# Layer 2's output gate computed ahead of its product, layer 3's first loads reordered, the last super chunk in halves

## The chip, the cores and the metric

The kernel runs on one core of one Trainium2 chip. The metric is the device time in microseconds (us) of the whole kernel, one launch, median of the runs shown. The engines are named as in the profile: PE is TensorE (matmuls), DVE is VectorE, ACT is ScalarE, POOL is GpSimd and SP is the engine whose queue issues nearly all DMAs here. All data are 32-bit floats; each fp32 matmul shows in the trace as two matmul records.

## The reference, cut to what matters

Four residual layers act on an image of 256 x 256 positions with 128 channels. Each is `x = x + layer(group_norm(x))`. Layer 0 is a triangle attention, layer 1 a triangle product with 16 channels; the change touches only layer 2 and the start of layer 3.

```python
# layer 2
zn = layernorm(z)                                   # over the 128 channels
a = sigmoid(zn @ Wga + bga) * (zn @ Wla + bla)
b = sigmoid(zn @ Wgb + bgb) * (zn @ Wlb + blb)
k = einsum('bimc,bmjc->bijc', a, b)                 # one 256 x 256 product per channel
out = sigmoid(zn @ Wgo + bgo) * (layernorm(k) @ Wlo + blo)
# layer 3: t is a 3x3 convolution of 128 channels to one
t = relu(conv(x, w1) + b1)
y = concat([x[:, :1], x[:, 1:] + t[:, :-1]], axis=1)
u = relu(conv(y, w1) + b1)
z = u + roll(y, 1, axis=1)                          # (two rows at the edge differ)
p = z, with relu(z @ w2c + b2) added, shifted along the width
q = relu(p @ w2c + b2) + p shifted                  # (two columns at the edge differ)
```

## The kernel before

Channels lie on the 128 partitions and the 65536 positions are cut into 32 super chunks (`NSC`) of 2048 (`SC`), each four matmuls wide (`CK` = 512). Between stages the data go through DRAM: `x2T` is layer 2's input, `aD` and `bD` are a and b, `kD` is k, `x3T` is layer 3's input. Layer 2 has three stages, and the code's names end in their numbers.

Stage 5 (lines 877 to 994) makes a and b. Per super chunk it runs 16 matmuls (`product5`, line 945), four sigmoids on ACT and four multiply-adds on DVE (line 976), and stores to `aD` and `bD`. The layer norm's factor is worked out a block of four super chunks at a time: `sums5` (PE), `root5`, a reciprocal, a store to `rs2D`, and `spread5`, which loads a row of `rs2D` broadcast over all partitions into `zns[s]`; `normalise5` then makes the normalised x there. The first block does this before the loop, with `fac` as its result (lines 950 to 962).

Stage 6 (lines 999 to 1054), the planes: `load6` loads four channels of a and b, `tri_turn` transposes (PE, then a copy on DVE), `tri_multiply` multiplies, and ACT, DVE and POOL copy the plane and keep its sum (`k1`) and sum of squares (`k2`). At the end `k1` and `k2` are turned into k's layer norm factor by three DVE steps, a square root on ACT and a reciprocal on DVE; the result goes through DRAM (`rkD`) to come back with one super chunk to a partition (`rk`). `rs2` is the same layout of stage 5's factor.

Stage 7 (lines 1057 to 1119), the output: `load7` loads k and x of a super chunk together, three ahead. `broadcast_rows` spreads a factor row over all partitions with four matmuls of 32 rows (line 860) into PSUM; `normalise_k` and `normalise_z` apply it on DVE, one super chunk ahead of use. Per half of a super chunk, `product7` makes the gate's matmuls and then those of k; ACT does the sigmoid, DVE the multiply-add. POOL adds the result to x for the whole super chunk (line 1116). `finish7` runs one super chunk later: two passes of ACT over x for the next group norm's sums (`g1`, `g2`) and the store to `x3T`.

Stage 9 (lines 1156 to 1419), layer 3: it works on chunks of 8 image rows (`load9`). The one-channel convolution goes round through DRAM: `taps` writes nine tap rows to `sD`, `load_block` loads them shifted (`p9_S`, for 16 rows), `sum_taps` makes t, `keep_t` stores it to `tD`, `load_t` loads it one row up, `image_u` and `image_e` make `e`, which goes to `eD` and back by `load_e` into `ers`. `finish_z` adds it to z. Two blocks, 0 and 1, are made before the loop; later ones are made inside it, a piece in each iteration. In an iteration, `p_half` and `q_half` are eight matmuls' worth of products with their DVE steps, and `emit` transposes and stores chunk s - 2.

Stages 5, 6, 7 and 9 stand under a manual schedule: the order on each engine is the order of the code. All DMAs of them but four are issued by SP, in the order of the code too; SP waits with an instruction until what it reads or overwrites is ready, and everything later on SP waits behind it. A tile pool that opens takes over memory of pools that were closed, and its first users wait for the last users of what lay there.

Of the kernel before, what the change touches and what calls it, by code (L numbers as in the profile page):

```python
# [15 lines left out]
P = 128  # L16
# [15 lines left out]
def kernel(ctx: ExitStack, tc: tile.TileContext, a: dict, out: bass.AP):  # L32
# [822 lines left out]
    def broadcast_rows(psX, rows, s, name):  # L855


        rb = [psX.tile([P, 2, CK], F32, name=name, tag="x") for _ in range(2)]
        for c in range(4):
            nc.tensor.matmul(  # L860
                rb[c // 2][:, c % 2, :], lhsT=sel[32 * c : 32 * c + 32, s : s + 1].to_broadcast([32, P]),
                rhs=rows[32 * c : 32 * c + 32, :], start=True, stop=True,
            )
        return [t.rearrange("p c t -> p (c t)") for t in rb]
# [5 lines left out]
    rs2_pool = rs2_scope.enter_context(tc.tile_pool(name="rs2", bufs=1))  # L870
    KB = 4
    BT = KB * SC
    with tc.tile_pool(name="p5", bufs=2) as sb, tc.tile_pool(name="p5psX", bufs=1, space=PSUM) as psX, tc.tile_pool(
# [4 lines left out]
        def load5(s):  # L878
            if s < NSC:
                xs[s] = sb.tile([P, SC], F32, name="p5_x", bufs=9)  # L880
                nc.sync.dma_start(xs[s], x2T[:, s * SC : (s + 1) * SC])
# [67 lines left out]

        for s in range(2 * KB):  # L950
            load5(s)
# [4 lines left out]
        fac = sb.tile([P, CK], F32, name="p5_fac", bufs=1)  # L956
        nc.vector.reciprocal(fac, var)
        store_block(rs2D, 0, fac)
        for s in range(2):
            spread5(s)  # L960
        normalise5(0)
        for s in range(NSC):
            b, j = divmod(s, KB)
            load5(s + 2 * KB)
# [26 lines left out]
            del zns[s]  # L991
            if j == 1 and (b + 1) * KB < NSC:
                compact5(b + 1, sums5(b + 1))


    rk = rs2_pool.tile([P, CK], F32, name="rk")
    rs2 = rs2_pool.tile([P, CK], F32, name="rs2_")
# [4 lines left out]
    with tc.tile_pool(name="p6", bufs=3) as sb, tc.tile_pool(name="p6s", bufs=1) as ssb, tc.tile_pool(  # L1002
        name="p6ps", bufs=3, space=PSUM
    ) as ps:
        k1 = ssb.tile([P, 2 * N], F32, name="p6_k1")
        k2 = ssb.tile([P, 2 * N], F32, name="p6_k2")
        nc.vector.memset(k1, 0.0)
        nc.gpsimd.memset(k2, 0.0)
        with tc.manual_schedule():
# [32 lines left out]

        nc.vector.scalar_tensor_tensor(k1, k1, -1.0 / D, k1, ALU.mult, ALU.mult)
        nc.vector.tensor_tensor(k2, k2, k1, ALU.add)
        nc.vector.tensor_scalar(k2, k2, 0.0, None, ALU.max)
        nc.scalar.activation(k2, k2, AF.Sqrt, bias=epst, scale=1.0 / D)
        nc.vector.reciprocal(k1, k2)
        nc.sync.dma_start(
            rkD.rearrange("o (p t) -> p (o t)", p=P), k1
        )  # L1050
        for c in range(4):
            nc.sync.dma_start(
                rk[32 * c : 32 * c + 32, :], rkD.rearrange("o (s c t) -> c (o s) t", c=4, t=CK)[c]
            )


    g1 = const.tile([P, NSC], F32, name="g1")
    g2 = const.tile([P, NSC], F32, name="g2")
    with tc.tile_pool(name="p7", bufs=2) as sb, tc.tile_pool(name="p7psX", bufs=2, space=PSUM) as psX, tc.tile_pool(
        name="p7psM", bufs=2, space=PSUM  # L1060
    ) as psM, tc.manual_schedule():
        ks, xs, kns, zns = {}, {}, {}, {}

        def load7(s):
            if s < NSC:
                ss = slice(s * SC, (s + 1) * SC)
                ks[s] = sb.tile([P, SC], F32, name="p7_k", bufs=4)
                nc.sync.dma_start(ks[s], kD[:, ss])
                xs[s] = sb.tile([P, SC], F32, name="p7_x", bufs=6)
                nc.sync.dma_start(xs[s], x2T[:, ss])  # L1070

        def normalise_k(s):
            rb = broadcast_rows(psX, rk, s, "p7_rk")
            kns[s] = sb.tile([P, SC], F32, name="p7_kn")
            for h in range(2):
                hs = slice(h * H2, (h + 1) * H2)
                nc.vector.tensor_tensor(kns[s][:, hs], rb[h], ks[s][:, hs], ALU.mult)
            del ks[s]

        def normalise_z(s):  # L1080
            rb = broadcast_rows(psX, rs2, s, "p7_rz")
            zns[s] = sb.tile([P, SC], F32, name="p7_zn")
            for h in range(2):
                hs = slice(h * H2, (h + 1) * H2)
                nc.vector.scalar_tensor_tensor(zns[s][:, hs], xs[s][:, hs], m2, rb[h], ALU.subtract, ALU.mult)

        def product7(src, w, h):
            pm = psM.tile([P, 2, CK], F32, name="p7_pm")
            for c in range(2):
                k = 2 * h + c  # L1090
                nc.tensor.matmul(pm[:, c, :], lhsT=w, rhs=src[:, k * CK : (k + 1) * CK], start=True, stop=True)  # L1091
            return pm.rearrange("p c t -> p (c t)")

        def finish7(s):
            junk = sb.tile([P, SC], F32, name="p7_j", bufs=1)
            nc.scalar.activation(junk, xs[s], AF.Identity, bias=m2neg, accum_out=g1[:, s : s + 1])
            nc.scalar.activation(junk, xs[s], AF.Square, bias=m2neg, accum_out=g2[:, s : s + 1])
            nc.sync.dma_start(x3T[:, s * SC : (s + 1) * SC], xs[s])
            del xs[s]

        for s in range(3):
            load7(s)
        normalise_k(0)
        normalise_z(0)
        for s in range(NSC):
            load7(s + 3)
            gt = sb.tile([P, SC], F32, name="p7_g")
            for h in range(2):
                hs = slice(h * H2, (h + 1) * H2)
                pg = product7(zns[s], wf2[:, 4, :], h)  # L1110
                nc.scalar.activation(gt[:, hs], pg, AF.Sigmoid, bias=b2w[:, 4:5])
                pl = product7(kns[s], w2c_[:, 5, :], h)
                nc.vector.scalar_tensor_tensor(gt[:, hs], pl, b2w[:, 5:6], gt[:, hs], ALU.add, ALU.mult)  # L1113
                if s + 1 < NSC:
                    (normalise_k if h else normalise_z)(s + 1)
            nc.gpsimd.tensor_tensor(xs[s], xs[s], gt, ALU.add)  # L1116
            if s:
                finish7(s - 1)
        finish7(NSC - 1)


# [41 lines left out]
    with tc.tile_pool(name="p9", bufs=2) as sb, tc.tile_pool(name="p9psM", bufs=2, space=PSUM) as psM, tc.tile_pool(  # L1163
# [167 lines left out]
        for s in range(2):  # L1331
            load9(s)
# [20 lines left out]
        for s in range(2, 4):  # L1353
            load9(s)
        sum_taps(-1)
        nc.sync.dma_start(image_rows(tD, 0, 1), blocks.pop(-1)["t"][P - 8 : P, 4 : 4 + BW])
        sum_taps(0)
        keep_t(0)
        load_t(0)
        image_u(0)  # L1360
        image_e(0)
        load_e(0)
        for s in range(2, 4):
            taps(xs[s], s * R, 4)
        load_block(1)
        for s in range(4, LEAD + 1):
            load9(s)
        finish_z(0)
        sum_taps(1)
        keep_t(1)  # L1370
        image_u(1)
        load_t(1)
        image_e(1)
        for s in range(4, LEAD):
            taps(xs[s], s * R, 4)
        load_e(1)
        load_block(2)
        load9(LEAD + 1)
        for s in range(NR + 2):
            load9(s + 8)  # L1380
            b = s // 2 + 2
            if s % 2 == 1 and b < NB:
                load_t(b)
            if s % 2 == 0 and 2 < b <= NB:
# [22 lines left out]
            if b < NB:  # L1407
# [6 lines left out]
            if s + LEAD < NR:  # L1414
                taps(xs[s + LEAD], (s + LEAD) * R, 4)
            if s % 2 == 1 and b + 1 < NB:
# [185 lines left out]
```

## Time and profile before

| what | us |
|---|---|
| median of 3 runs (3517.76 to 3522.11) | 3517.95 |
| the profiled execution's own time | 3521.85 |
| its span | 3520.2 |
| stage 5's loop, PE busy throughout | 492.7 |
| stage 6's loop, PE busy 290.95 of | 291.8 |
| stage 7's loop, PE busy 300.16 of | 300.4 |
| from the end of stage 7's loop to the ninth stage's third chunk | 81.2 |
| the rest of stage 9, PE busy 337.56 of | 357.0 |

The times are sums over windows of the trace, read at the points where the chain of waits changes stage. The profile is of one execution, so a difference between two kernels is made between two profiled executions, and the medians say how large the difference is. PE's busy time counts matmuls as the trace's model places them; a window that is busy throughout is one in which PE's order alone sets the pace.

Over the whole span PE is busy for 3123.1 us (89%), DVE for 2318.3, ACT for 1956.9 and POOL for 1611.1.

### The profile page before, as it was taken

The numbers are of one execution on the slowest core, as the hardware profiler recorded it, in microseconds if no ns is written. First come the engines' busy times: TensorE is split into PE (matmuls) and PEld (weight loads), VectorE is DVE, ScalarE is ACT, GpSimd is POOL, SyncE is SP. The second block draws the span as 40 slices with busy tenths as digits, with TensorE's granted clock in tenths as the row PEclk, the third lists the DMA queues.
The fourth block names the chain that finished last, engine by engine and source line by source line (L and its number), as shares of the span: only waits on it lengthen the run. The fifth ranks groups of instructions, "written<-read, shape, count | busy, mean of one in ns | idle before, by whom it ended". The sixth has DMA issues, their size and how long they took to land.

```text
span 3520.2 us, 52462 instructions
## 1 busy us (share of the span) xinstructions
PE 3123.1 (89%) x20268; PEld 1648.5 (47%) x20268; DVE 2318.3 (66%) x2638; ACT 1956.9 (56%) x2194; POOL 1611.1 (46%) x822
## 2 busy tenths in 40 slices
PE   4565999999999999965597899999999899949998
PEld 3512555555555555521432344443899433314444
DVE  4623888888888888852398354544555577737776
ACT  3563777777777777733243454443444366636655
POOL 4002777777777777732497000000555344414343
PEclk7887999999999999979798899999999899969999
DMA  9883333333333333349599586765999788647664
GB/s 333 322 304 123 98 121 110 110 122 112 107 122 115 105 121 115 108 162 380 175 342 343 224 314 249 278 262 197 351 350 350 291 333 336 263 167 204 194 193 136
DMA packets 309867, 760.54 MB, mean 216 GB/s; under 512 B 77627, under 2 KB 148957, under 8 KB 259181
## 3 DMA queue, kind: packets, MB, share of 16 engines
q1 hardware_dynamic: 298749, 747.48, 60.4%
q0 software_dynamic: 10864, 9.65, 0.9%
q8 instruction: 162, 2.65, 0.3%
q14 instruction: 92, 0.75, 0.1%
HBM read 469.33 MB, written 287.66 MB: 215 GB/s over the span
## 4 chain that ended last, share of the span: by engine, by line
PE 39%; DMA 7%; DVE 2%; ACT 1%; POOL 1%; SPq 1%; issue 0%; ACTq 0%; DVEq 0%; POOLq 0%
PE p_pm L945 13%; PE p_pm L1091 7%; PE tp_z L1560 6%; PE p_pm L1286 5%; PE tp_a L1549 2%; DMA p_x<-x1T 2%; DMA x2T<-p_x 1%; PE p_st L902 1%; PE p_pt L1323 1%; PE p_rz L860 1%; PE p_rk L860 1%; PE p_eb L860 1%; PE p_pp L1179 1%; PE p_pg L810 1%; POOL p_x L827 1%; DMA p_t<-tD 0%
## 5 line engine op out<-in xcount | busy, mean ns | idle before, releaser
L489 DVE TENSOR_TENSOR p_e<-p_S,triT 128x1024 f32<-128x1024 f32 x512 | 609.4, 1212 | 144.6 <-PE p_S L479 144.6
L499 POOL TENSOR_TENSOR p_es<-p_e 128x1024 f32<-128x1024 f32 x256 | 603.4, 2368 | 127.0 <-issue 67.2
L497 ACT ACTIVATE p_e<-p_e,mbT 128x1024 f32<-128x1024 f32 x512 | 551.9, 1138 | 63.1 <-DVE p_e L489 61.3
L945 PE MATMUL p_pm<-p_zn,wf 128*128 128x512 f32 x1024 | 444.3, 596 | 15.8 <-DVE p_zn L938 15.8
L464 PE MATMUL p_mm<-p_xn,wf 128*128 128x512 f32 x768 | 409.1, 617 | 9.2 <-POOL p_xn L437 9.2
L437 POOL TENSOR_TENSOR p_xn<-p_xn,p_rs 128x1024 f32<-128x1024 f32 x64 | 153.5, 2399 | 455.0 <-DMA p_x<-xT 262.7
L945 PEld LDWEIGHTS p_pm<-p_zn,wf 128*128 128x128 f32 x1024 | 194.9, 191 | 265.4 <-issue 244.8
L479 PE MATMUL p_S<-p_q,p_k 32*128 32x256 f32 x4096 | 295.4, 400 | 5.0 <-DVE p_e L489 5.0
L479 PEld LDWEIGHTS p_S<-p_q,p_k 32*128 32x128 f32 x4096 | 185.8, 184 | 161.5 <-PE p_mm L455 91.7
L1300 POOL TENSOR_TENSOR p_q<-p_q,p_pb 128x2024 f32<-128x2024 f32 x32 | 144.2, 4507 | 252.8 <-DVE p_pb L1294 183.8
L1560 PE MATMUL tp_z<-p_B,tp_at 128*128 128x256 f32 x1024 | 250.5, 388 | 0.6 <-DMA p_B<-bD 0.3
L512 PE MATMUL p_o<-p_e,p_v 128*32 128x256 f32 x4096 | 249.2, 384 | 0.0
L1116 POOL TENSOR_TENSOR p_x<-p_x,p_g 128x2048 f32<-128x2048 f32 x32 | 145.4, 4545 | 181.0 <-DVE p_g L1113 181.0
L1037 POOL TENSOR_TENSOR p_k<-p_k,p_sq 128x512 f32<-128x512 f32 x128 | 163.1, 1274 | 135.5 <-ACT p_sq L1035 135.5
L999 POOL DMA_DIRECT2D rs__17992<-rs2D x4 | 2.1, 520 | 468.7 <-DMA rs2D<-p_vc 468.7
L1560 PEld LDWEIGHTS tp_z<-p_B,tp_at 128*128 128x128 f32 x1024 | 185.2, 191 | 22.9 <-DVE tp_at L1551 1.4
L464 PEld LDWEIGHTS p_mm<-p_xn,wf 128*128 128x128 f32 x768 | 126.7, 191 | 114.5 <-issue 90.2
L1036 DVE TENSOR_TENSOR p_k<-tp_z,p_k 128x512 f32<-128x512 f32 x128 | 88.6, 692 | 127.0 <-ACT p_sq L1035 127.0
L512 PEld LDWEIGHTS p_o<-p_e,p_v 128*32 128x32 f32 x4096 | 120.4, 110 | 110.1 <-ACT p_g L470 41.5
L1033 ACT COPY p_K<-tp_z 128x512 f32<-128x512 f32 x128 | 75.1, 586 | 165.5 <-PE tp_z L1560 165.5
L976 DVE SCALAR_TENSOR_TENSOR p_b<-p_pm,b2w,p_b 128x1024 f32<-128x1024 f32 x64 | 82.2, 1284 | 125.9 <-PE p_pm L945 111.6
L455 PEld LDWEIGHTS p_mm<-wf,p_xn 128*128 128x128 f32 x1024 | 135.4, 193 | 62.9 <-issue 61.9
(342 smaller groups left out, 5890.8 us busy)
## 6 DMA issues: line engine op xcount, KB each, us to landing
p_x<-x2T SPq DMA_DIRECT2D x64, 1024.0 KB
p_x<-x1T SPq DMA_DIRECT2D x48, 1024.0 KB
p_x<-in_x_dram SPq DMA_DIRECT2D x32, 1024.0 KB
p_x<-xT SPq DMA_DIRECT2D x64, 512.0 KB
p_rs<-rsD SPq DMA_DIRECT2D x64, 512.0 KB
p_rb<-rzD SPq DMA_DIRECT2D x256, 128.0 KB
x1T<-p_x SPq DMA_DIRECT2D x64, 512.0 KB
p_zn<-rs2D SPq DMA_DIRECT2D x32, 1024.0 KB
```

The source lines that it names most:

```text
L437: nc.gpsimd.tensor_tensor(xn, xn, t["rs"], ALU.mult)
L464: nc.tensor.matmul(pm, lhsT=w, rhs=t["xn"][:, cs_], start=True, stop=True)
L479: nc.tensor.matmul(Ss[h // 2][:, h % 2, u, :], lhsT=t["k"][hp, r * N + u * P : r * N + (u + 1) * P], rhs=t["q"][hp, r * N : (r + 1) * N], ...
L489: nc.vector.tensor_tensor(e[:, :, 2 * p : 2 * p + 2, :].rearrange("p u h n -> p h u n"), Ss[p], triT[:, 2 * p : 2 * p + 2, :, :], ALU.add,)
L497: nc.scalar.activation(e[:, u, :, :], e[:, u, :, :], AF.Exp, bias=mbT[:, u, i : i + 1])
L499: nc.gpsimd.tensor_tensor(es, e[:, 0, :, :], e[:, 1, :, :], ALU.add)
L512: nc.tensor.matmul(t["o"][hp, r % 2, :], lhsT=t["v"][:, r * 2 + u, hp], rhs=e[:, u, h, :], start=(u == 0), stop=(u == 1),)
L945: nc.tensor.matmul(pm[:, c, :], lhsT=wf2[:, i, :], rhs=zns[s][:, k * CK : (k + 1) * CK], start=True, stop=True)
L1037: nc.gpsimd.tensor_tensor(k2, k2, sq, ALU.add)
L1091: nc.tensor.matmul(pm[:, c, :], lhsT=w, rhs=src[:, k * CK : (k + 1) * CK], start=True, stop=True)
L1286: nc.tensor.matmul(pm[:, 2 * c : 2 * c + 2, :], lhsT=w2c, rhs=src[:, r : r + 2, :], start=True, stop=True)
L1560: nc.tensor.matmul(pz[:, t, :], lhsT=at[:, u, t * P : (t + 1) * P], rhs=Bc[:, u, :], start=(u == 0), stop=(u == 1))
```

## The change

Stage 5: the first block's factor stays in `var` and is still stored, but super chunk 0 is normalised from a PE broadcast of it (`broadcast_rows` into the pool `p5_pm`), and only chunk 1's is loaded at that point. Seven buffers hold x in place of nine. The tiles of the last two super chunks' gates are taken outside the stage, and after the loop their gates are computed from `zns[30]` and `zns[31]`.

Stage 6: `rk`, `rs2`, `k1` and `k2` have a pool of their own; the loads of x for super chunks 0 to 2 are issued after the last three stores of k, into a pool that lies outside the stage's.

Stage 7: k and x are loaded apart, k three ahead and x five ahead (seven buffers in two pools). The gate of super chunk s + 3 is computed in iteration s, and not for the last two; gates 0 to 2 and the normalised x of 0 to 3 are made ahead of the loop, between the steps of k's factor. `normalise_k` works in place. The last sums go over the gate's tile as their scrap output. The last super chunk is added on DVE, summed and stored in halves.

Stage 9: four loads of x stand at the front; only block 0 is made ahead of the loop, and blocks 1 and 2, each from the first step to the last, in iterations 0 and 1, with the taps that belong to them.

```diff
+    gates = {s: rs2_pool.tile([P, SC], F32, name=f"gate_{s}") for s in (NSC - 2, NSC - 1)}
...
-                xs[s] = sb.tile([P, SC], F32, name="p5_x", bufs=9)
+                xs[s] = sb.tile([P, SC], F32, name="p5_x", bufs=7)
...
         var = sums5(0)
         root5(var)
-        fac = sb.tile([P, CK], F32, name="p5_fac", bufs=1)
-        nc.vector.reciprocal(fac, var)
-        store_block(rs2D, 0, fac)
-        for s in range(2):
-            spread5(s)
-        normalise5(0)
+        nc.vector.reciprocal(var, var)
+        store_block(rs2D, 0, var)
+        spread5(1)
+        zns[0] = sb.tile([P, SC], F32, name="p5_zn", bufs=3)
+        for h, rb in enumerate(broadcast_rows(psM, var, 0, "p5_pm", tag="p5_pm")):
+            hs = slice(h * H2, (h + 1) * H2)
+            nc.vector.scalar_tensor_tensor(zns[0][:, hs], xs[0][:, hs], m2, rb, ALU.subtract, ALU.mult)
...
+        for s in gates:
+            for h in range(2):
+                nc.scalar.activation(
+                    gates[s][:, h * H2 : (h + 1) * H2], product5(s, 4, h), AF.Sigmoid, bias=b2w[:, 4:5]
+                )
...
+                    if q >= D // 4 - 3:
+                        load7x(q - (D // 4 - 3), x7_pool, 3)
...
+        normalise_z(0)
+        nc.vector.scalar_tensor_tensor(k1, k1, -1.0 / D, k1, ALU.mult, ALU.mult)
+        nc.vector.tensor_tensor(k2, k2, k1, ALU.add)
+        nc.vector.tensor_scalar(k2, k2, 0.0, None, ALU.max)
+        nc.scalar.activation(k2, k2, AF.Sqrt, bias=epst, scale=1.0 / D)
+        normalise_z(1)
+        nc.vector.reciprocal(k1, k2)
+        nc.sync.dma_start(rkD.rearrange("o (p t) -> p (o t)", p=P), k1)
+        for c in range(4):
+            nc.sync.dma_start(rk[32 * c : 32 * c + 32, :], rkD.rearrange("o (s c t) -> c (o s) t", c=4, t=CK)[c])
+        gate7(0, 0)
+        gate7(0, 1)
+        normalise_z(2)
+        gate7(1, 0)
+        gate7(1, 1)
+        normalise_z(3)
+        gate7(2, 0)
+        gate7(2, 1)
         normalise_k(0)
-        normalise_z(0)
         for s in range(NSC):
-            load7(s + 3)
-            gt = sb.tile([P, SC], F32, name="p7_g")
+            load7k(s + 3)
+            load7x(s + 5, *((x7_pool, 3) if (s + 5) % 7 < 3 else (sb, 4)))
+            last = s == NSC - 1
             for h in range(2):
                 hs = slice(h * H2, (h + 1) * H2)
-                pg = product7(zns[s], wf2[:, 4, :], h)
-                nc.scalar.activation(gt[:, hs], pg, AF.Sigmoid, bias=b2w[:, 4:5])
-                pl = product7(kns[s], w2c_[:, 5, :], h)
-                nc.vector.scalar_tensor_tensor(gt[:, hs], pl, b2w[:, 5:6], gt[:, hs], ALU.add, ALU.mult)
-                if s + 1 < NSC:
-                    (normalise_k if h else normalise_z)(s + 1)
-            nc.gpsimd.tensor_tensor(xs[s], xs[s], gt, ALU.add)
-            if s:
-                finish7(s - 1)
-        finish7(NSC - 1)
+                gate7(s + AHEAD, h)
+                pl = product7(ks[s], w2c_[:, 5, :], h)
+                nc.vector.scalar_tensor_tensor(gts[s][:, hs], pl, b2w[:, 5:6], gts[s][:, hs], ALU.add, ALU.mult)
+                if h:
+                    normalise_k(s + 1)
+                else:
+                    normalise_z(s + AHEAD + 1)
+                if last:
+                    nc.vector.tensor_tensor(xs7[s][:, hs], xs7[s][:, hs], gts[s][:, hs], ALU.add)
+                    if h == 0:
+                        finish7(s - 1)
+                    sums7(xs7[s][:, hs], gts[s][:, hs], s + h)
+                    nc.sync.dma_start(x3T[:, s * SC + h * H2 : s * SC + (h + 1) * H2], xs7[s][:, hs])
+            del ks[s]
+            if not last:
+                nc.gpsimd.tensor_tensor(xs7[s], xs7[s], gts[s], ALU.add)
+                if s:
+                    finish7(s - 1)
...
-        for s in range(2):
+        for s in range(4):
             load9(s)
...
         load_block(0)
-        for s in range(2, 4):
-            load9(s)
         sum_taps(-1)
...
+        image(0)
         for s in range(2, 4):
             taps(xs[s], s * R, 4)
-        load_block(1)
-        for s in range(4, LEAD + 1):
+        for s in range(4, 6):
             load9(s)
         finish_z(0)
-        sum_taps(1)
...
-        for s in range(4, LEAD):
-            taps(xs[s], s * R, 4)
-        load_e(1)
-        load_block(2)
-        load9(LEAD + 1)
+        load_block(1)
+        for s in range(6, 8):
+            load9(s)
         for s in range(NR + 2):
...
-            if b < NB:
+            if s < 2:
+
+                image(s + 1)
+                for i in range(2):
+                    taps(xs[4 + 2 * s + i], (4 + 2 * s + i) * R, 4)
+                load_block(s + 2)
+            elif b < NB:
```

`gate7(s, h)` is `product7` of the normalised x with a sigmoid, for super chunks 0 to 29; `image(b)` is `sum_taps`, `keep_t`, `load_t`, `image_u`, `image_e` and `load_e` of block b in that order; `load7k` and `load7x` are the two halves of `load7`.

## The prediction

> **What bounds the kernel now.** I read the windows view first (busy time by stage; I took the stage borders from the chain of waits), then the chain of waits around each border, then the timeline at the borders. The windows, one line for each stage that the change touches and the seams between them:
>
> ```profile
> 1931.00:1963.30 32.30, 11.36 (x69) 2.65 (x69) 7.93 (x9) 14.59 (x10) 0.00 (x0) 0.61 0.84 337
> 1963.30:2456.00 492.70, 492.70 (x1472) 208.75 (x1472) 239.77 (x179) 221.29 (x183) 2.06 (x4) 0.99 0.67 249
> 2456.00:2467.20 11.20, 0.14 (x2) 0.04 (x1) 1.77 (x2) 0.00 (x0) 0.53 (x1) 0.69 0.79 287
> 2467.20:2759.00 291.80, 290.95 (x1536) 262.27 (x1536) 164.41 (x255) 137.95 (x255) 161.80 (x127) 0.99 0.91 337
> 2759.00:2781.60 22.60, 6.52 (x17) 2.78 (x17) 10.23 (x9) 2.91 (x4) 1.28 (x2) 0.61 0.62 233
> 2781.60:3082.00 300.40, 300.16 (x1008) 111.75 (x1008) 225.89 (x189) 192.28 (x186) 140.94 (x31) 1.00 0.84 319
> 3095.40:3163.20 67.80, 33.73 (x123) 9.48 (x123) 27.62 (x49) 16.64 (x19) 10.68 (x8) 0.65 0.56 184
> ```
>
> Columns: window, length, busy us of PE, PE weight loads, DVE, ACT, POOL, then granted TensorE clock, DMA share, GB/s. The loops of layer 2 (lines two, four and six) are TensorE from end to end; the seams have 11, 23 and 68 us with TensorE mostly idle. Matmul work taken out of a loop and put in a seam is therefore worth its full time, as long as the seam does not grow. What each seam waits for, from the chain of waits:
>
> ```profile
> 1956.17 4.70 DMA p_zn<-rs2D
> 1960.89 2.36 DVE p_zn L938
> ...
> 2457.55 4.24 DMA bD<-p_b
> 2462.44 6.90 DMA p_B<-bD
> ...
> 2763.90 3.36 DVE p_k L1047
> 2767.28 2.00 DMA rkD<-p_k
> 2771.25 5.03 DMA p_k<-kD
> 2777.93 3.21 PE p_rz L860 x8
> ...
> 3083.29 4.51 POOL p_x L1116
> 3087.82 3.85 DMA x3T<-p_x
> ```
>
> All are round trips through DRAM and single vector instructions.
>
> [...] matmuls at 1963.3 start 0.85 us apart for about 5 us, then 0.43 us. [...] the small store to tD issued at 3133.45, behind three 1 MB loads, took 6.71 us, while the 256 KB store to rkD took 2.00 us. [...]
>
> **The change part by part.** Unless a row is named, times are of the timeline before.
>
> (a) Start of the a/b loop: block 0's factor is spread by four matmuls instead of store and broadcast load. Before: reciprocal ends 1953.61, first product 1963.30. After: the broadcast runs from 1953.7 (a cold group of 8 takes 3.28 us, its first half about 1.7), the first 1024-column normalise is 1.2 us, so the product can start at about 1956.8. Gain 6.5 us; [...] I take 7. Seven x buffers instead of nine: a load is still issued about 20 us before its square, against 5 us of transfer, hidden by 13.8 us of products per super chunk (cost if uncovered: 5 us once per block).
>
> (b) Gates of super chunks 30 and 31 after the last product (2456.1): 16 pass records x 0.43 = 6.9 us of TensorE, to 2463.0. The built order shows the first load of A (2462.06 before) waiting for the last of these matmuls, because it takes their zn buffer. So the plane stage starts 1.0 us later; [...] I take +1.
>
> (c) Seam between planes and output loop. DVE now does normalise_z(0) ahead of the k sums, and in the built order that waits for the last kD store, whose buffer zn takes: issued 2759.6, landed about 2764.4 [...]. Then 2.46 + 2.3 (three sums steps) + 2.46 (normalise_z(1)) + 3.35 (reciprocal): the store to rkD is issued near 2775, eight later than before. Behind it on DVE are normalise_z(2), (3) and normalise_k(0). But SP has by then queued k0, k1, k2, x3, x4 [...]. So rkD lands about 2781 and rk about 2783, before 2771.4. Gates 0 to 2 with four broadcasts (3 x 3.63 + 4 x 1.07 = 15.2 us) fill TensorE between 2761 and 2782. The loop's own rhythm then starts at 2784; before it was 2783.0 (from 2787.71 less half an iteration of 4.70). I take +1; bounds -1 ([...] gate 2 is then last) and +6 (rk lands at 2788).
>
> (d) Loop. An iteration is 9.40 us of TensorE: gate 3.63, product 3.63, two broadcasts 1.07 each. Iterations 0 to 25 keep that. 26 drops one broadcast; 27 to 31 have only product and one broadcast, 4.70 us. There a chain becomes late: second product half ends, +0.24, STT 1.21, first half of normalise_k 1.17, +0.1, next product, and two product halves 3.8: 6.5 us per iteration. POOL 4.54, ACT 4.2 fit under it. End of the last product after loop start: 26 x 9.40 + 7.3 + 5 x 6.5 = 284.2, before 298.7. Gain 14.5. The ring must carry 87 MB-sized transfers in that time, 321 GB/s, as now (319). x(s+5) is issued some 2.5 us into iteration s (it waits ACT's sums of s-2), lands near 8, is used at 12.7.
>
> (e) Last super chunk in halves: before, from the last product (3081.8) to the last sum (3092.04): 10.2 us. After: POOL's add of chunk 30 ends 0.2 us before the last product; ACT then has 4.1 us of chunk 30's sums and two halves of about 2.3 us (estimate from 2.0 us per 2048 columns and 0.19 per accumulator read): 8.5. ACT, not POOL, is last. Gain 1.7. DVE's adds (about 1.2 each, from the 1.17 row) lie beside it.
>
> (f) Layer 3's start, with T = the end of gn_rstd (3095.5). SP now issues x0 to x3 first, so the tap stores of chunk 1 wait for x3 (T+13.3): the first S loads go at T+15.6, before T+12.7. In exchange t's store has no x load ahead of it (4.78 us before, 2 now): e of image 0 is ready at T+25.3 in both, the first product at T+32 instead of T+44. Then image 1 is late: its S load sits behind x4, x5 (lands T+41; before T+36), its t store behind x6 to x8 (lands T+49.5). DVE waits in order at image_e(1) to T+51, with p_half(1) behind it, and TensorE waits for e until T+54.5. Image 2, inline too, holds DVE to T+69. By this walk q_half(1) starts at T+70.6 (before T+72.5), S of block 3 lands T+79.8, and q_half(2) starts T+84.3 (before T+83.6). The 12 us gained at the front are spent on the two inline round trips: +1 in sum. Bounds: -12 (the small transfers do not wait behind the loads) and +10 (each of the two images one 5 us hop worse). Afterwards the order is as before, 11.03 us per chunk.
>
> Sum: -7 + 1 + 1 - 14.5 - 1.7 + 1 = -20.2 us. The profiled execution took 3521.85 us (span 3520.2), 3.9 above the median; the sum is made on it: 3501.7. On the median of 3517.95 it is 3497.8; I predict 3498.
>
> **The rivals.** 1. Layer 3's start keeps its gain: [...] image 1's transfers are quicker than I make them. For it: TensorE is idle half of that window (33.7 of 67.8 us). Against: the 6.71 us store. Then -20.2 - 11: 3486. 2. Only part of the gate's time comes back: rk arrives at 2788 (+5) or, in the tail, loads and stores limit (2 MB per 6.5 us is 323 GB/s; at 280 it is 7.5 us, +5): 3508. Against: windows with 337 GB/s. 3. Slower: the inline images. Iterations 0 and 1 each hold DVE through store, load, store, load of one image; at the longest hops seen (S 5.2, tD 6.7, then as many loads ahead as SP has issued, 8 us for three) an image takes 35 us with only 7 us of products beside it, and layer 3 starts near T+100 instead of T+72.5. That is +27 in place of +1: about 3524. It decides from about 27 us lost there; below that the loop's 14.5 and the front's 7 win. 4. The gates hide nothing since the seams grow by as much: needs +15 in (c), rk at 2798; [...]. About 3512 to 3517.
>
> **How the numbers follow.** A measurement here can tell about 0.2% (7 us) from no change. Forecast (3491 to 3504) 0.50; rival 1 (3478 to 3491) 0.20; rival 2 (3504 to 3511) 0.14; rival 4 0.06; rival 3 0.10. Range: 3482 to 3510, which leaves out rivals 3 and 4 and the far end of rival 1. Faster 0.84, same 0.06, slower 0.10.
>
> **What would show it.** (a): first product about 3 us after the reciprocal. (b): first transposes about 1 us later after the last a/b product. (c): the rkD store landing only when x4 has; loop start 25 us after the last plane's matmul. (d): gate-free iterations of about 6.5 us at the end, 9.40 ahead of them. (e): ACT back to back at the end. (f): first product near T+32, but q_half(2) near T+84, with DVE waiting for t2 twice. It is wrong if the 9.40 rhythm breaks (x loads late), or if T to q_half(2) moves by over 10 us.

## The result, and the profile after

The changed kernel takes 3503.39 us (median of 4 runs, 3499.27 to 3504.92), the kernel before 3517.86 on the same chip (4 runs, 3510.86 to 3522.11): a ratio of 0.9959, 95% interval 0.9941 to 0.9977. That is 14.5 us less; the forecast was 20 less, at 3498. The profiled executions differ by more, 3503.97 against 3521.85 us. The 17.9 us between them, stretch by stretch:

| stretch of the trace | before | after | difference | forecast |
|---|---|---|---|---|
| start to 1/std of gn2 (unchanged code) | 1933.1 | 1925.6 | -7.6 | 0 |
| (a) 1/std of gn2 to the first a/b product | 30.2 | 22.5 | -7.6 | -7 |
| first to last a/b product | 492.8 | 492.1 | -0.7 | 0 |
| (b) last a/b product to the first tp_z | 13.4 | 16.1 | +2.7 | +1 |
| first to last tp_z | 287.3 | 287.3 | 0.0 | 0 |
| (c) last tp_z to the start of the output loop | 26.2 | 29.1 | +2.9 | +1 |
| (d) output loop to its last product | 298.7 | 295.9 | -2.9 | -14.5 |
| (e) last product to the last sum | 10.3 | 8.9 | -1.4 | -1.7 |
| (f) T (end of gn3's 1/std) to p_half of chunk 4 | 89.8 | 90.7 | +0.9 | +1 |
| the rest of layer 3 (unchanged code) | 334.9 | 330.8 | -4.1 | 0 |

Here gn2 and gn3 are the group norms ahead of layers 2 and 3, 1/std is the end of the reciprocal that completes their statistics, `tp_z` are the products of the planes, and "the last tp_z" is the start of their last group of matmuls. Row (d) counts the loop before from 2783.0, as the prediction does. The 3.4 us from the last sum to T, the same in both, are in no row.

The total looks like the forecast, but it is not made of the forecast's parts, and that it came close is luck. The largest term, (d), gave 2.9 us instead of 14.5, and 11.7 us come from code that is the same in both kernels.

The windows view of the changed kernel, with the same seven stretches as before the change; columns as there (window, length, busy us of PE, PE weight loads, DVE, ACT and POOL, clock, DMA share, GB/s):

```profile
1925.50:1948.10 22.60, 12.24 (x75) 3.11 (x75) 6.81 (x10) 13.05 (x8) 0.00 (x0) 0.73 0.69 288
1948.10:2440.20 492.10, 492.10 (x1473) 208.84 (x1474) 240.90 (x180) 221.32 (x183) 0.00 (x0) 1.00 0.68 254
2440.20:2452.40 12.20, 6.87 (x17) 2.69 (x15) 1.77 (x2) 4.46 (x4) 2.58 (x5) 0.92 0.72 259
2452.40:2745.50 293.10, 290.93 (x1536) 262.24 (x1536) 164.46 (x255) 137.79 (x254) 161.36 (x127) 0.99 0.94 344
2745.50:2772.60 27.10, 20.90 (x65) 7.50 (x64) 15.48 (x13) 10.81 (x11) 1.53 (x2) 0.81 0.85 327
2772.60:3068.30 295.70, 284.64 (x932) 105.33 (x928) 215.50 (x180) 183.09 (x175) 140.66 (x31) 0.99 0.83 302
3080.80:3149.30 68.50, 39.33 (x139) 12.56 (x139) 30.63 (x53) 21.99 (x25) 10.73 (x8) 0.72 0.54 182
```

The gates did move: PE is now busy for 6.87 us in the seam of line three (0.14 before) and 20.90 in that of line five (6.52 before). Line six is the surprise. The output loop has 932 matmul records where it had 1008, as planned, and yet it is only 4.7 us shorter between the borders shown, and the transfers run at 302 GB/s where they ran at 319. PE's busy time there, 284.64, is too high to be work alone. This is the same loop in the last run in which a store is issued ahead of a load (it is described below):

```profile
2781.90:3065.20 283.30, 275.70 (x932) 102.45 (x928) 215.55 (x180) 183.19 (x176) 140.77 (x31) 1.00 0.84 316
```

Its 932 records are busy for 275.70 us, so the other 9 us in line six are pauses that count as busy; and 7.6 us without a busy PE are left in this run too. What PE waits for stands in the chain of waits of the changed kernel (start, us, what was waited for):

```profile
2927.82 3.65 PE p_pm L1098 x8
2932.98 4.55 POOL p_x L1163
2937.55 9.37 DMA x3T<-p_x
2947.40 11.26 DMA x3T<-p_x
2959.13 11.44 DMA x3T<-p_x
...
3006.24 11.11 DMA x3T<-p_x
3017.42 8.89 DMA p_x<-x2T
3030.09 5.36 PE p_pm L1098 x12
```

From 2937 to 3026 us the chain is no longer PE's. It goes from one store of x to the next, seven in a row, the last six of them 11.1 to 11.4 us long, and then through a load of x. The timeline of SyncE's queue shows how that begins (start, duration of the issue, engine, line, what is issued):

```profile
2918.75 0.32 SPq L1116 DMA_DIRECT2D x3T<-p_x  x1
2922.08 0.32 SPq L1075 DMA_DIRECT2D p_k<-kD  x1
2925.62 0.32 SPq L1021 DMA_DIRECT2D p_x<-x2T  x1
2928.15 0.32 SPq L1116 DMA_DIRECT2D x3T<-p_x  x1
2931.49 0.32 SPq L1075 DMA_DIRECT2D p_k<-kD  x1
2936.01 0.32 SPq L1021 DMA_DIRECT2D p_x<-x2T  x1
2937.55 0.32 SPq L1116 DMA_DIRECT2D x3T<-p_x  x1
2940.89 0.32 SPq L1075 DMA_DIRECT2D p_k<-kD  x1
2946.98 0.32 SPq L1021 DMA_DIRECT2D p_x<-x2T  x1
2947.40 0.38 SPq L1116 DMA_DIRECT2D x3T<-p_x  x1
2950.29 0.32 SPq L1075 DMA_DIRECT2D p_k<-kD  x1
2958.72 0.32 SPq L1021 DMA_DIRECT2D p_x<-x2T  x1
2959.13 0.38 SPq L1116 DMA_DIRECT2D x3T<-p_x  x1
2959.69 0.32 SPq L1075 DMA_DIRECT2D p_k<-kD  x1
2970.64 0.32 SPq L1021 DMA_DIRECT2D p_x<-x2T  x1
```

With seven buffers and loads five ahead, the load of x of s+5, issued in turn s of the loop, takes the buffer of s-2, so it waits for the store of s-2 to land. On the queue the store of s-1 stands behind that load. Up to 2925.62 this costs nothing: loads and stores each come every 9.40 us and the store lands in time. The load of 2936.01 comes 10.39 us after its predecessor, and from the next turn on each store is issued 0.4 us behind a load, lands some 11 us later, and lets the next load go only then. The period is now the landing time of a store and not PE's 9.40 us: some 11.7 us a turn. The last four lines show a full turn of it: load, store and the next load of k are issued within 1 us, and then nothing until the store has landed. Their 3 MB are 9.4 us at the 334 GB/s that the loop reaches without this (an estimate from the windows views further down), and in what is left of the turn the transfers thin out: the DMA share there is 0.79, and 0.89 without. Each turn uses up some 2.3 us of the lead by which x is loaded ahead of its use, and when that is gone PE is late too; the first such group on PE's timeline:

```profile
2969.57 2.32 PE L860 MATMUL p_rk<-rk,sel 32*128 32x512 f32 x8 [0.51 <-DVE p_zn L1090]
```

Its eight records, four matmuls, wait for VectorE's scaling of x, which waits for x: 0.51 us ahead of them, and another 1.2 us between them, since the group takes 2.32 us and otherwise 1.14. I call this the lock, and this theory T1. Its rival T2 is that the loop's transfers simply go no faster.

### The profile page after: what moved, and what is told of

The parts are those of the page before. It is cut to its first block, busy times and chain, and to the rows that moved or that the text cites. A ratio compares the mean times of both kernels' runs of the same rounds, so it can differ in the third digit from the quotient of the medians.

```text
span 3502.3 us, 52445 instructions
## 1 busy us (share of the span) xinstructions
PE 3131.9 (89%) x20260; PEld 1652.7 (47%) x20260; DVE 2316.9 (66%) x2637; ACT 1962.3 (56%) x2198; POOL 1604.9 (46%) x821
## 5 line engine op out<-in xcount | busy, mean ns | idle before, releaser
L1054 POOL TENSOR_TENSOR k<-k,p_sq 128x512 f32<-128x512 f32 x128 | 162.9, 1273 | 135.2 <-ACT p_sq L1052 135.2
L1163 POOL TENSOR_TENSOR p_x<-p_x,p_g 128x2048 f32<-128x2048 f32 x30 | 136.2, 4540 | 177.8 <-DVE p_g L1150 146.9
L1053 DVE TENSOR_TENSOR k<-tp_z,k 128x512 f32<-128x512 f32 x128 | 88.5, 691 | 128.5 <-ACT p_sq L1052 128.5
```

Source lines behind the costliest of these rows:

```text
L1054: nc.gpsimd.tensor_tensor(k2, k2, sq, ALU.add)
```

## The experiments

In what follows the "stretch of products" is from the first product with k to the last one's end: 1.8 us shorter than row (d) of the table, since it leaves out the gate's half ahead of it. It is 296.9 us before and 294.0 in the first profile after. "Store first" means that the store is issued ahead of the load of x, as in the first of these runs. Times of runs are compared on the same chip: the first four with each other, then four, then three, then the last. The kernel before took 3520.08, 3523.72, 3523.91 and 3522.14 us (medians) on these four chips.

**The store ahead of the load, and eight buffers.**

```diff
-            load7x(s + 5, *((x7_pool, 3) if (s + 5) % 7 < 3 else (sb, 4)))
...
                 if s:
                     finish7(s - 1)
+            load7x(s + 5, *((x7_pool, 3) if (s + 5) % 7 < 3 else (sb, 4)))
```

> The changed kernel with one edit in the output loop: SyncE issues the store of super chunk s-1 ahead of the load of x of s+5 instead of behind it. T1 (a lock of store and load: that load waits until the store of s-2 has landed, because it takes its buffer, and the next store stands behind the load, so that from 2936 us on one store and one load follow each other every 11.5 us): the stores are then no longer held, loads of x are issued every 9.4 us to the end, PE does not stall between 3017 and 3042 us, and the stretch from the loop's start to its last product falls from 295.7 to about 285 us (the forecast's own size), the total from 3503 to about 3492. T2 (the transfers of the loop, 3 MB in each of its turns, go no faster with the wider lead of the loads, whatever the order of issue): the stretch stays at 294 to 297 and the total at 3503; loads stay 11 us apart. T3 (the lost time is in the seams or in the loop's last five turns): the stretch stays, and the stall at 3017 moves by less than 3 us.

```diff
-            load7x(s, sb, 4)
+            load7x(s, sb, 5)
...
-            load7x(s + 5, *((x7_pool, 3) if (s + 5) % 7 < 3 else (sb, 4)))
+            load7x(s + 5, *((x7_pool, 3) if (s + 5) % 8 < 3 else (sb, 5)))
```

> The changed kernel with eight buffers of x in the output loop instead of seven, order of issue unchanged: the load of x of s+5 then takes the buffer of s-3, whose store was issued a whole turn earlier. T1 (lock of store and load through the shared buffer): the load finds its buffer free, loads and stores go every 9.4 us, the stretch from the loop's start to its last product falls from 295.7 to about 285 us and the total from 3503 to about 3492. T2 (the transfers themselves are the limit): 294 to 297 and 3503. If the order of issue on SyncE alone is to blame and not the buffer, this run stays and the one with the store first falls.

Measured: 281.4 us for the stretch of products in both, loads every 9.40 us to the end, 3497.69 and 3500.54 us (3492 was expected of both). T2 falls: 3 MB in a turn of 9.40 us do go through. So does T3, by which the stretch would have stayed. T1 is not proved by these two, since the next two did not touch the loop and were not locked either.

**Layer 3's old head; stage 5's old start.** The first has lines 1375 to 1468 of the changed kernel in the form before. The second:

```diff
         store_block(rs2D, 0, var)
-        spread5(1)
-        zns[0] = sb.tile([P, SC], F32, name="p5_zn", bufs=3)
-        for h, rb in enumerate(broadcast_rows(psM, var, 0, "p5_pm", tag="p5_pm")):
-            ...
+        for s in range(2):
+            spread5(s)
+        normalise5(0)
```

> The changed kernel with the first loads and images of layer 3 in the order of the kernel before; all else as changed. The forecast: the reorder costs 1 us, so from the last 1/sqrt of stage 7's variance to the first p_half of super row 4 this run takes 89.8 (the changed kernel 90.7) and the total is 1 us lower, 3502. Rival 1 (the reorder keeps what it gains at the first product, 13 us earlier): this run loses 8 to 12 us, total 3511 to 3515.

> The changed kernel with the start of stage 5 as before: the first super chunk's scale goes out to memory and back as a broadcast instead of through PE, seven buffers of x kept. The forecast: the stretch from 1/std of gn2 to the first product goes back from 22.5 to about 29.5 to 30.2 us (+7), total 3510. Rival (the gain is covered, since stage 5 is limited by its transfers or engines afterwards): the stretch grows by 7, but the products that follow, first to last 492.1 us, take that much less, and the total stays at 3503.

Measured, old head: T to p_half of chunk 4 takes 91.8 us; with the new head it was 90.7 at first and 90.2 to 92.6 in eleven other profiles. The total is 3498.29, between the two runs above. So the reorder neither costs nor gains more than about 2 us, and rival 1 is out: its 8 to 12 us are not there. Old start: from 1/std of gn2 to the first product 29.1 us (22.5 in the first profile after, 21.0 to 24.0 in the others), with the products behind it unchanged, and 3510.13 us, 10 to 12 above the other three. The gain of (a) is real and is not given back. Some 6 us of the difference stand in the trace; why the medians differ by more is open.

In both the stretch of products took 281.4 us: the loop as changed, without a lock. The wait of SyncE's queue for the store, in total, times and longest, for the first profile after and for the run with the old head:

```profile
SPq L1021 <- DMA x3T<-p_x: 111.6, 25, 10.6
```

```profile
SPq L1021 <- DMA x3T<-p_x: 44.6, 25, 4.1
```

The load waits for a store in 25 turns in both. At 1.8 us each that is harmless; at 4.5 on average it is the lock. In the run with the old head one load came 0.9 us late, at 2980.27, and the next was on time again; in the first profile after, one came 1.0 late and none was on time any more.

**The changed kernel again, and the lock provoked.** One run is the changed kernel unaltered. In the next two a megabyte is loaded once, in turn 8, to a buffer that nothing reads, without and with the store ahead of the load:

```diff
+        more = sb.tile([P, SC], F32, name="p7_more", bufs=1)
         for s in range(NSC):
             load7k(s + 3)
...
+            if s == 8:
+                nc.sync.dma_start(more, x2T[:, 0:SC])
```

> The changed kernel once more, unaltered. In its first profile the stretch from the output loop's first product of layer 2's second factor to its last took 294.0 us with loads and stores locked every 11.5 us from 2936 us on; the four runs so far, two of which leave the loop alone, took 281.4 us in each case and were never locked. T1a (the lock is entered by chance, when one store lands more than some 7 us after its issue, and then stays): a run without it takes 281.4 us, with loads every 9.4 us to the end, and the total lies near 3497 to 3500; a run with it 290 to 300 us. T1b (the changed kernel's own order always locks, and the two runs with an old head or an old start escaped because of their changed places in memory): 294 us again, locked from about the same turn. T2 (limit of the transfers): 294.

> The changed kernel with one more load of 1 MB, from the first super chunk of x to a buffer that nothing reads, issued in turn 8 of the output loop (near 2860 us) just ahead of that turn's store of x. At some 340 GB/s it delays what follows by 3 us, once. T1a (a single late store enters a lock that holds to the loop's end): loads and stores are 11.3 to 11.8 us apart from turn 9 or 10 on, eight turns earlier than in the first profile of the changed kernel, PE stalls sooner, and the stretch of products takes 305 to 315 us, some 25 to 30 more than the undisturbed 281.4. A queue that recovers: loads are back at 9.4 us within a turn or two, and the stretch takes 281.4 to 285.

> The same extra load of 1 MB in turn 8, with the store of s-1 issued ahead of the load of x of s+5. T1a (the lock needs the store behind the load that waits for the store before it): no lock, loads every 9.4 us a turn later, the stretch of products 281.4 to 284 us. If the extra megabyte itself costs the time, this run is as slow as the one with the order of the changed kernel.

Measured: the unaltered kernel 293.3 us, locked, and from the same turn (161.6 us after the first product with k). With the extra load 313.7 us, 32 more than undisturbed, and 3534.34 us against 3505.05. With the extra load and the store first 281.4 us and 3506.04 us. SyncE's queue in the run with the extra load:

```profile
2857.32 0.32 SPq L1021 DMA_DIRECT2D p_x<-x2T  x1
2857.69 0.42 SPq L1147 DMA_DIRECT2D p_more<-x2T  x1
2859.85 0.32 SPq L1116 DMA_DIRECT2D x3T<-p_x  x1
2863.19 0.32 SPq L1075 DMA_DIRECT2D p_k<-kD  x1
2870.08 0.32 SPq L1021 DMA_DIRECT2D p_x<-x2T  x1
2870.50 0.38 SPq L1116 DMA_DIRECT2D x3T<-p_x  x1
2872.59 0.32 SPq L1075 DMA_DIRECT2D p_k<-kD  x1
2878.92 0.32 SPq L1021 DMA_DIRECT2D p_x<-x2T  x1
2879.34 0.38 SPq L1116 DMA_DIRECT2D x3T<-p_x  x1
2881.99 0.32 SPq L1075 DMA_DIRECT2D p_k<-kD  x1
2890.41 0.32 SPq L1021 DMA_DIRECT2D p_x<-x2T  x1
2890.82 0.38 SPq L1116 DMA_DIRECT2D x3T<-p_x  x1
```

The load that follows the extra one waits for its store to 2870.08, 10.2 us after that store's issue. The next gap is 8.8, and from then on it is 11.5 to 12.2 us in all turns but the last. One megabyte is some 3 us of transfer at 334 GB/s (an estimate); it cost 32 us against the undisturbed loop. A delay that comes once thus turns into one that stays, and the store's place behind the load is what keeps it. (With the store first, the extra load stands 5.7 us ahead of the store and not 2.2, so there it may disturb less to begin with.)

**The seams.** The store first, and besides it rs2 loaded at channel 16 of the planes instead of ahead of them, and the k sums finished ahead of the first scaling of x (the lines of this last edit):

```diff
-        normalise_z(0)
         nc.vector.scalar_tensor_tensor(k1, k1, -1.0 / D, k1, ALU.mult, ALU.mult)
...
-        normalise_z(1)
         nc.vector.reciprocal(k1, k2)
+        normalise_z(0)
+        normalise_z(1)
```

> The store first as before, and two edits at the seams. (b) The four loads of rs2 on GpSimd's queue move from ahead of the planes to channel 16 of the planes: if they are what makes the first B land 8.6 us after its issue instead of 6.9, the time from the end of the gates of 30 and 31 to the first tp_z falls from 9.0 to 9.8 us to some 7.5 to 8; if not it stays. (c) The sums of k are finished on VectorE ahead of the scaling of x of super chunk 0, which waits 4.2 us for a store of k: rkD then goes out some 3 to 5 us earlier. If the round trip of rk sets the loop's start, the time from the last tp_z to the first product with k falls from 30.6 to 30.9 us to 26 or 27; if the gates of 0 to 2 on PE set it, as the profile suggests (the broadcasts of rk do not wait), it stays within 1 us. Total: 3494 to 3497, the best so far.

Measured: (b) the end of the gates to the first tp_z takes 8.0 us (9.0 to 9.8 in nine other profiles, 9.15 in the first after), so the four loads on GpSimd's queue do delay the first B, which now lands 7.41 us after its issue (8.57 in the first after). (c) missed both ways: from the last tp_z to the first product with k 33.4 us, 2.6 more than without the edit. The gates on PE set the loop's start, and they wait for the scaling, which now stands behind the k sums and the reciprocal. 3502.56 us, where 3494 to 3497 was expected.

The first run of the next group keeps the store first and the late loads of rs2, puts the k sums back and gives the first scaling a buffer that was not the planes':

```diff
+        zns[0] = rk_pool.tile([P, SC], F32, name="zn0")
         normalise_z(0)
```

> Store first and the late loads of rs2 as in the run before, the sums of k again behind the scaling of x of super chunk 0 as in the changed kernel, and that scaling's output in a buffer of its own (8 KB per partition kept from before the planes) in place of one that lies where the planes' buffers were, which made it wait 4.2 us for a store of k. If the gates of 0 to 2 on PE, in their order after this first scaling, set the loop's start, the time from the last tp_z to the first product with k falls from 30.6 to 31.1 us by 3 to 4, to some 27; the loop takes 281.4, the time from the end of the gates of 30 and 31 to the first tp_z stays near 8. If the next user of the old buffers (the scaling of super chunk 1, or the first gate's output) only inherits the wait and was late by as much, it stays at 29.5 to 31. Total 3 to 5 us below the run with only the store first.

> The changed kernel unaltered, a third profile, and timed on the same chip as the next one. Both profiles so far entered the lock in turn 16 (161.6 us after the first product with k). If it always enters there: 293 to 294 us for the stretch of products again, and a median 8 to 13 us above the run with the store first. If it is a matter of chance: 281.4 us, and medians that differ by less.

> Only the store ahead of the load of x, once more, on the same chip as the unaltered kernel: 281.4 us for the stretch of products with loads every 9.4 us, and a median 8 to 13 us below the unaltered kernel's if that one always locks; the same median within 3 us if the unaltered kernel's lock is rare.

Measured: the unaltered kernel is locked a third time, 293.3 us, 3506.54 us. The store first: 281.4 and 3501.38. The windows of the first profile after, then of the last store-first run, cut at the same distances from the loop's start:

```profile
2772.60:2926.00 153.40, 153.40 (x523) 57.33 (x520) 117.73 (x98) 97.35 (x94) 70.55 (x16) 1.00 0.87 322
2926.00:3018.00 92.00, 89.29 (x280) 32.60 (x280) 62.05 (x52) 53.78 (x51) 38.42 (x9) 0.96 0.79 274
```

```profile
2781.90:2935.30 153.40, 153.40 (x523) 57.33 (x520) 117.69 (x98) 97.33 (x94) 70.53 (x16) 1.00 0.85 318
2935.30:3027.30 92.00, 92.00 (x316) 33.99 (x315) 70.36 (x59) 61.04 (x59) 43.40 (x11) 1.00 0.89 334
```

For 153 us the two loops do the same 523 matmul records. In the next 92 us the locked one does 280, the other 316, and the transfers run at 274 and 334 GB/s: they are slower because they wait for each other, not because they are full. PE's busy time, 89.29 of 92, hides this, since pauses inside a group count as busy; the count of instructions shows it. A window that is busy nearly throughout is therefore not yet one in which PE's order alone sets the pace.

The difference of the medians, 5.2 us, is under half of the 11.9 between the two traces. Perhaps not every run of the changed kernel is locked, though all three profiles are; its 22 runs spread from 3491 to 3527 us, the 5 with the store first from 3498 to 3504. The run with the extra load points the same way: its trace is 20 us longer in the loop than that of the unaltered kernel on its chip (313.7 against 293.3), its median 29 us above. How often the unaltered kernel locks when no profile is taken stays open.

The scaling's own buffer gave 29.7 us from the last tp_z to the first product with k, 1.2 less and not 3 to 4: its wait fell from 4.16 to 1.26 us, but rk became last. The median, 3500.99 us, is 0.4 below that of the run with only the store first, not 3 to 5. SyncE's queue there:

```profile
2759.84 1.27 SPq L1076 DMA_DIRECT2D p_k<-kD  x3
2761.16 1.15 SPq L1017 DMA_DIRECT2D p_x<-x2T  x2
2767.18 0.32 SPq L1133 DMA_DIRECT2D rkD<-k  x1
2775.43 1.72 SPq L1135 DMA_DIRECT2D rk<-rkD  x4
```

rk's loads are issued when rkD has landed, 8.25 us after its issue (5.35 in the changed kernel, where it was issued 2.8 us later). It lands at the same time after the last tp_z: at 23.3 us in the changed kernel, at 23.4 here, and at 23.5 in the run with the k sums first, where it had been issued at 10.5. Five loads of 1 MB are ahead of it in all three. The last run moves two of them behind:

```diff
-        for s in range(3):
-            load7k(s)
+        load7k(0)
...
             nc.sync.dma_start(rk[32 * c : 32 * c + 32, :], rkD.rearrange("o (s c t) -> c (o s) t", c=4, t=CK)[c])
+        for s in range(1, 3):
+            load7k(s)
```

> The run with the scaling's own buffer, and one edit more: the loads of k of super chunks 1 and 2, 1 MB each, are issued behind the round trip of rk instead of ahead of it. In the run before, rkD went out 15.1 us after the last tp_z instead of 17.9, and yet landed after 23.4 (23.3 in the changed kernel), with 5 MB of loads issued ahead of it. If those transfers set the time at which it lands, it now lands some 6 us earlier (2 MB at about 340 GB/s), the broadcasts of rk do not wait, the gates' own chain on PE is last, and the time from the last tp_z to the first product with k falls from 29.7 to 26 to 27.5 us. If the round trip has a fixed length, it stays at 29 to 30. The stretch of products stays at 281.4, and the time is the lowest of all, about 3 us below the run before, a difference that the medians alone may not show.

```profile
2747.63 0.32 SPq L1076 DMA_DIRECT2D p_k<-kD  x1
2748.00 0.90 SPq L1017 DMA_DIRECT2D p_x<-x2T  x2
2754.95 0.32 SPq L1132 DMA_DIRECT2D rkD<-k  x1
2758.13 1.72 SPq L1134 DMA_DIRECT2D rk<-rkD  x4
```

rkD now lands after 3.18 us, and the seam takes 27.2 us, as expected of transfers that set it. This run has the lowest median, 3492.72 us, a ratio of 0.9923 to the kernel before on its chip, interval 0.9906 to 0.9940; that of the run with only the store first (0.9935, 0.9922 to 0.9949) overlaps it.

## Why the prediction was right, and where not

(a) Right. Forecast -7; the first product came 3.5 us after the reciprocal (3.2 forecast), and over the twelve profiles with the new start the stretch fell from 30.2 to 23.3 us on average. Undoing it cost 6 us in the trace and 10 to 12 in the median.

(b) +2.7 for +1. The load of A waits for the last gate matmul, 1.0 us later, as forecast. The rest was left out: the four rs2 loads on GpSimd's queue, which no longer stood ahead of the seam, now run beside the first B, which lands 8.57 us after its issue instead of 6.90. How the transfers of the two queues share the time is not shown; what the runs show is its length: in the three runs with those loads moved, the end of the gates to the first tp_z took 7.6 us on average, in the ten others 9.4.

(c) +2.9 for +1. The walk to rk was right: rkD was issued 17.9 us after the last tp_z (18.2 forecast) and landed at 23.3 (24.2 forecast, from my own estimate of the loads ahead of it). But the gates on PE were last, not rk. PE had stood idle for 4.30 us, from 2748.57 to 2752.87, and from there to 2759.0 the clock granted was 0.50, and 1.00 from 2762.15 on. The broadcast ahead of the first gate took 3.27 us where I put 1.07 (in part it waits for VectorE between its halves: the weights of the second half load at 2754.06, when VectorE's scaling is done), and the gate of super chunk 0 took 6.15 where I put 3.63; the next, at the clock of 1.00, took 3.70. I reckoned with a slow first group in (a) and not in this seam. What sets the length of the slow stretch is not shown: in the two runs with the scaling's own buffer PE stood idle for 1.40 us there, and the gate of super chunk 0 still took 5.77 and 5.31.

(d) **This is the step that failed**: forecast -14.5, measured -2.9 in the first profile, and -3.6 in each of the two more of the same kernel. Its matmul count was right: in the nine profiles without a lock, the loop takes 283.2 us (281.4 and 1.8), 15.5 less than before, against 284.2 forecast; the last iterations took 6.28 us where 6.5 stood. What failed is the sentence on x: "x(s+5) is issued some 2.5 us into iteration s (it waits ACT's sums of s-2), lands near 8". It names one of the two readers of the buffer. The other is the store of s-2, issued 6.9 us earlier, which landed some 5.4 us after its issue on average (3.66 us to the start of the wait and 1.8 of it, in the run with the old head), and the store of s-1 stands behind the load on the same queue. So the slack was 1.5 us and not the 12.7 - 8 of the load's own arrival; when one landing used it up (7.8 to 8.0 us after the store's issue in the three locked profiles of the unaltered kernel) the loop fell into a period of some 11.7 us. The prediction named the sign itself: "It is wrong if the 9.40 rhythm breaks (x loads late)". Bandwidth, which rival 2 and my check of 321 GB/s on SyncE's queue (the "ring" of the forecast) were about, was never the limit: 334 GB/s ran.

(e) -1.4 for -1.7, with ACT back to back as forecast; the half sums were 1.13 us a pass.

(f) Right in its total and nearly so in its steps: the first product at T+30.9 (32 forecast), q_half(1) at T+68.4 (70.6), q_half(2) at T+82.6 (84.3). The 13 us gained at the first product were gone by the third chunk, as written.

So the total of the first pair was close by luck, for two reasons that offset each other: the lock cost 12.6 us, and unchanged code ran 11.7 us faster in that pair of executions. Averaged over the profiles of the kernels after, against the one of before, leaving out for each term the runs that edit it, the terms without a lock are -6.9 + 2.9 + 2.9 - 15.5 - 1.4 + 1.3 = -16.7 us where -20.2 was forecast, and unchanged code makes 5 more (2.7 up to gn2, 2.1 in the rest of layer 3). The two medians with only the store first, 22.4 and 22.5 below the kernel before on their chips, agree with that sum, though the traces of before in it are those of one execution. The unaltered kernel's later medians are 18.7 and 17.4 below.

## What to carry to other kernels

When a load is moved further ahead, list everything that still uses the buffer it takes, the store too, and look at what stands behind that load on its queue: if it is the store that the next load will wait for, one late landing can set the period. Issue the store first, or have one more buffer; here the loop took 281.4 us with either, and 293.3 to 294.0 in the three locked profiles of the unaltered kernel. And when a stage's rate drops, compare counts of instructions and GB/s at equal distances from its start: busy shares hardly show it (PE was busy for 89.29 of 92.00 us in the locked stretch, with 280 records where the other had 316).

## What had not been expected of the hardware

- This loop, with the same work in each turn, ran at two stable rates, 9.40 and about 11.7 us a turn. A load 0.9 us late was followed by recovery, one 1.0 late by the lock; one extra megabyte moved it over. Why the unaltered kernel had its late store in the same turn in three profiles, and two kernels with the same loop did not lock, stays open.
- A store of 1 MB that was issued 0.4 us behind a load of 1 MB, with a load of k 0.5 to 2.9 us behind it, landed 11.1 to 11.4 us later in the first profile after, about twice the average of 5.4 of one that had 2.5 us between them.
- The same instructions from the start to 1/std of gn2 took from 1924.0 to 1937.5 us in the 13 profiles of the kernels after, so a few us of two totals can't be put down to an edit without looking at the stretch that it is in.
